# A four-layer stack on one Trainium2 core: image 1's first layer laid beside image 0's spline and attention, and a planner with other prices for TensorE

## The chip, the cores and the metric

The kernel runs on one core of a Trainium2 chip. The metric is the device time in microseconds of one execution, lower is better; the time before is 17189.96 us, the median of three runs (17174.03 to 17196.51).

## What is computed

An input of 32 images, each 128 channels by 56 x 56 pixels in float32, goes through four layers. Each adds its result to its input, and each first normalises its input over groups of four channels (`_gn`). Cut to what matters:

```python
# layer 0: a 1x1 convolution whose weights are mixed per image, then three depthwise convolutions
pooled = x.mean(axis=(2, 3)); attn = softmax(fc2(relu(fc1(pooled))) / 34)
y = einsum('boi,bihw->bohw', einsum('bk,koi->boi', attn, dw_weight), x) + attn @ dw_bias
out = sum(silu(depthwise3x3(y, dilation=d) + ds_bias) for d in (1, 3, 5))
# layer 1: a cubic B-spline of ten coefficients, the same for every element
basis = bspline_basis(clip(x, -2, 2), knots); out = einsum('...n,n->...', basis, coeffs)
# layer 2: linear attention over channels (8 heads, keys and queries from an 8x8 pooled image), depthwise 3x3
out = depthwise3x3(linear_attn(relu(pooled @ Wq.T), relu(pooled @ Wk.T), Wv x)) + bp
# layer 3: a Mamba block: layer norm, projections, convolution over 4, and a state space scan
h = exp(delta * A) * h + delta * B * xc      # 3136 steps, 16 states for each of 256 channels
y = sum_n(h * C) + xc * D;  out = out_proj(y * silu(z))
```

Images don't depend on each other. Within an image the layers follow each other, and the scan of layer 3 goes through the pixels in order.

## The kernel before

**Tiles.** An image is a tile `xt` of 128 channels by 3136 pixels; three such tiles rotate. Work is cut into seven chunks of 448 pixels (`CH`). The scan of a chunk takes 16 steps (`STEPS`): a step multiplies `du` with the B rows (`h<-du,pb`, VectorE), scans twice (`h<-da,last,h`, VectorE), multiplies by the C rows (`hc<-h,cb`, GpSimd) and sums over the states (`y<-hc,sums`, TensorE, added up in PSUM). The decay `da` is an Exp on ScalarE. `pb` is a float32r matmul into a PSUM tile with one buffer (`ps_bc`); `da` has three, `hc` two, and all other matmuls share the three buffers of `mm`.

**Stages.** A front part (lines 1256 to 1262) takes image 0 through layers 0, 1, 2 and the scan's first inputs, and image 1 through layer 0. Then a loop of five passes runs, each of six images, and after it two images are written out at the end. While the scan of image b runs, layers 1 and 2 of image b+1 (`until_scan`) and layer 0 of image b+2 (`first_layer`) are mixed in. Generators yield after each piece of work with its rough price, and `Pieces` doles the pieces out over the scan's 112 steps in proportion to those prices.

**Layer 0** (`dynamic_conv`) writes the mixed 1x1 convolution with a border to a DRAM image `padded[0]` and reads it back as stacks: for each chunk and dilation three shifted copies of the rows, laid over the partitions, and a row of ones for the bias. A stack is four DMAs on SyncE's queue (three of 264 KB and one of 8.2 KB), then twelve small matmuls (`mm<-stack,dsT`, four at a time in column groups), a Tanh (`t<-mm`, ScalarE), a product (`g`, VectorE) and an addition (`xt<-xt,g`, GpSimd). **Layer 1** (`spline`) reads each chunk as 16 DMAs of 56 KB (`stack<-xt`), makes hat functions on ScalarE (`hats`, one buffer) and sums them with 28 column-group matmuls in three groups (`mm<-hats,wspl`); two of the sums are squared on ScalarE (`sq`). **Layer 2** (`linear_attention`) has a chain of small matmuls (`wkT`, `wqT`, `wv`, then `bv`, `nm` and `kb` with 1 or 2 columns), eight heads that write `padded[1]`, and stacks of its own. All stacks of the three layers share one pool of three buffers (`stk`).

**The order.** `Plan` records every operation as a `Work` instead of issuing it (`add`), with the regions it reads and writes and a price in microseconds (`price`). `order` gives each work a due time: its scan step times 4.5 us, less its lead (`ahead`), or earlier where something due depends on it. `attempt` then plays the program forward with one clock for each engine: again and again it takes the work that can start first, of those of one engine the one that is due first, and sets that engine's clock on by the price. It lets no work be over 12 steps (`WINDOW`) ahead of the oldest undone one. `issue` writes all works out in the order of their planned starts, so each engine gets a fixed list that it follows in order; semaphores, not the plan's clock, decide when an instruction really runs. Every planned instruction carries line 325, where `issue` calls it, so the profile tells groups apart by tile names. The price of a matmul in the kernel before is in line 171:

```python
w.cost += max(0.06, n * (5e-4 if args[2].dtype == F32R else 1.8e-3))
```

where `n` is the number of columns. The plan is made once for the front, once for the loop's body and once for the last two images. `Pieces.finish` (line 1167) runs a generator to its end; with a plan it sets the step up by one for each piece.

Of the kernel before, what the change touches and what calls it, by code (L numbers as in the profile page):

```python
# [14 lines left out]
F32R = mybir.dt.float32r  # L15
# [4 lines left out]
P = 128  # L20
# [60 lines left out]
class Work:  # L81


    __slots__ = ("engine", "calls", "reads", "writes", "cost", "bytes", "step", "ahead", "table", "due", "next",
                 "ready", "fresh")

    def __init__(self, engine, step, ahead):
        self.engine, self.step, self.ahead = engine, step, ahead
        self.calls, self.reads, self.writes = [], [], []
        self.cost = self.bytes = self.ready = self.due = 0.0  # L90
        self.table = None
        self.next, self.fresh = [], []


class Plan:
# [6 lines left out]
    RATE, LANDING = 2e5, 1.8  # L102
    TABLE = 1.28
    NEVER = 1e18
    PATIENCE = {"tensor": 0.5, "scalar": 0.9, "gpsimd": 0.6, "vector": 0.1, "sync": 0.0}

    def __init__(self, nc, tc):
# [55 lines left out]
    def price(self, w, engine, method, args, kw):  # L163

        n = args[0].free_size()
        if method == "dma_start":
            w.cost += 0.35
            w.bytes += 4 * n * args[0].partition_size()
        elif engine == "tensor":
            n = args[2].free_size() if method == "matmul" else n  # L170
            w.cost += max(0.06, n * (5e-4 if args[2].dtype == F32R else 1.8e-3))
        elif engine == "scalar":
            if method == "activation" and args[2] in (AF.Exp, AF.Tanh, AF.Ln):
                w.table = "ln" if args[2] == AF.Ln else "exp"
            columns = sum(isinstance(kw.get(k), bass.AP) for k in ("bias", "scale"))
            w.cost += 0.06 + 8.34e-4 * n + 0.09 * columns + 0.03 * (args[1].space != bass.MemoryType.PSUM)
        elif engine == "gpsimd":
            if n <= 8:
                w.cost += 0.52 if ALU.pow in args else 0.15
            else:  # L180
                slow = method != "tensor_scalar" or ALU.add not in args
                w.cost += 0.14 + n * (1.2e-3 if not slow else 2.12e-3 if method != "tensor_scalar" else 3.8e-3)
        elif method == "tensor_tensor_scan":
            w.cost += 0.11 + 2.085e-3 * n
        else:
            if method == "tensor_reduce" or method == "bn_stats":
                n = args[1].free_size()
            w.cost += 0.08 + 1.02e-3 * n
# [54 lines left out]
    def attempt(self, born, behind):  # L243
# [6 lines left out]
        left = dict(self.uses)  # L250
        free = {e: 0.0 for e in self.PATIENCE}
        ready = {e: [] for e in self.PATIENCE}
        slots, held, table, bus, first = {}, {}, None, 0.0, 0
        for name, (pool, tag, bufs) in self.tiles.items():
            slots[pool, tag] = [0.0] * bufs
            held[pool, tag] = []
# [5 lines left out]
        while len(out) < len(works):  # L262
# [4 lines left out]
            for e, cand in ready.items():  # L267
                for i in cand:
                    w = works[i]
                    if w.step > front:  # L270
                        continue
                    at = max(w.ready, free[e])
                    for name in w.fresh:
                        at = max(at, min(slots[self.tiles[name][:2]], default=self.NEVER))
                    if at >= self.NEVER:
                        continue
# [11 lines left out]
            key, e, i, at = best  # L288
            w = works[i]
            ready[e].remove(i)  # L290
            done[i] = True
            for name in w.fresh:
                t = self.tiles[name][:2]
                slots[t].remove(min(slots[t]))
                held[t].append(name)
            free[e] = at + w.cost
            if w.table:
                free[e] += self.TABLE * (w.table != table)
                table = w.table
            end = free[e]  # L300
            if w.bytes:
                bus = max(bus, end) + w.bytes / self.RATE
# [12 lines left out]
                    ready[v.engine].append(k)  # L315
            out.append((at, i))
        return [i for _, i in sorted(out)]

    def issue(self):
        order, works = self.order(), self.works  # L320
# [29 lines left out]
def tile_conv_stack(ctx: ExitStack, tc: tile.TileContext, out: bass.AP, x: bass.AP, w: dict):  # L350
# [3 lines left out]
    plan = Plan(nc, tc)  # L354
# [770 lines left out]
    def first_layer(src, b):  # L1125

        xt = xts[b % 3]
        for j in range(NCH):
            nc.sync.dma_start(xt[:, j * CH : (j + 1) * CH], src[:, j * CH : (j + 1) * CH])
        yield from dynamic_conv(xt, sts[b % 2])  # L1130

    def until_scan(b):

        xt = xts[b % 3]
        st = yield from spline(xt, sts[b % 2])
        st = yield from linear_attention(xt, st)
        norm = carried[b % 2]
        norm_weights(st, *norm)
        yield 5.0
        layer_norm(xt, xns[b * NCH % 3], 0, norm)  # L1140
        yield 5.0

    def first_inputs(b):
        return ssm_inputs(xts[b % 3], b * NCH, carried[b % 2])
# [6 lines left out]
    class Pieces:  # L1151
# [12 lines left out]
            except StopIteration:  # L1164
                self.gen = None

        def finish(self, plan=None):
            while self.gen is not None:
                if plan is not None:
                    plan.at(plan.step + 1)  # L1170
                self.next()
            return self.taken

    xv = x.rearrange("b c l -> c b l")
# [79 lines left out]

    totals = [0.0, 0.0]
    plan.start()
    for b in range(2):
        totals[0] = Pieces(first_layer(xv[:, b : b + 1, :].squeeze(1), b)).finish(plan)
        if b == 0:
            totals[1] = Pieces(until_scan(0)).finish(plan)  # L1260
            Pieces(first_inputs(0)).finish(plan)
    plan.issue()
    with tc.For_i(0, B - 2, unroll) as i:
        images(i, unroll, True)
# [103 lines left out]
```

## Time and profile before

| | |
|---|---|
| median of three runs | 17189.96 us |
| profiled execution | 17194.07 us, its span 17192.1 us |
| busy: TensorE, VectorE, ScalarE, GpSimd | 14998.2, 14452.2, 11730.3, 10788.9 us |
| mean granted TensorE clock | 0.885 |
| first scan step (`h<-du,pb`) starts at | 508.6 us |
| images 0 to 29 (front's scan start to the last pass's end) | 508.6 to 16260.5 us, 525 us each |
| image 30, image 31 | 502.0 us, 429.6 us to the end of the span |

The profile is one execution. Busy time is given for each engine; TensorE's matmuls and weight loads (PEld) are told apart. A window row gives, for a stretch of the span, each engine's busy time with the number of its instructions, the granted TensorE clock as a share of full speed, and the share of the 16 DMA engines' time in use with GB/s. A wait row `A x <- B y` says how long engine A sat idle before its instruction on tile x until B's instruction on y released it. A float32 matmul stands as two records, a float32r matmul as one.

### The profile page before, as it was taken

To read this page: it belongs to the slowest core of one execution; us is meant where nothing else is said; L and a number is where in the kernel's file an instruction comes from. 1 tells how busy PE (TensorE), PEld (TensorE's weight loads), DVE (VectorE), ACT (ScalarE), POOL (GpSimd) and SP (SyncE) were. 2 spreads that over 40 slices of the span, in tenths; PEclk is the share of its full clock that TensorE was granted. 3 is DMA by queue.
4 is the path that set the end of the run, shared out by engine and by line. 5 is a ranking of instruction groups with operands and counts; after the bars stand their busy time and mean duration, and the time that the engine had idled before them with its cause. 6 is when DMAs were issued, how large, how long until landed. Compare 5 with 4: busy or idle time off the path is not lost. (4 is left out here: it accounts for less than half of the span.)

```text
span 17192.1 us, 216067 instructions
## 1 busy us (share of the span) xinstructions
PE 14998.2 (87%) x68192; PEld 4866.0 (28%) x68192; DVE 14452.2 (84%) x17314; ACT 11730.3 (68%) x21127; POOL 10788.9 (63%) x6406
## 2 busy tenths in 40 slices
PE   6888998888988888988889888889888898888888
PEld 1222222222222222222222222222222222222222
DVE  2788888888888888888888888888888888888889
ACT  3666677766677666777666776667776667766675
POOL 1566666666666666666666666666666666666666
PEclk7888898989998888989899888899888999888887
DMA  4443443434433444434344334444343443344421
GB/s 105 105 96 94 101 98 84 98 89 97 106 89 87 96 96 97 100 84 98 91 96 106 93 82 96 95 102 98 85 97 88 98 106 91 85 98 95 94 55 31
DMA packets 986167, 1590.09 MB, mean 92 GB/s; under 512 B 175621, under 2 KB 611208, under 8 KB 984330
## 3 DMA queue, kind: packets, MB, share of 16 engines
q1 hardware_dynamic: 985002, 1576.06, 39.0%
q8 instruction: 548, 8.98, 0.2%
q14 instruction: 617, 5.05, 0.1%
HBM read 785.62 MB, written 173.18 MB: 56 GB/s over the span
## 5 line engine op out<-in xcount | busy, mean ns | idle before, releaser
L325 POOL TENSOR_TENSOR hc<-h,cb 128x896 f32<-128x896 f32 x3584 | 7480.6, 2092 | 5035.7 <-DVE h L325 2490.3
L325 DVE TENSOR_TENSOR_SCAN h<-da,last,h 128x448 f32<-128x448 f32 x6144 | 6811.5, 1138 | 628.5 <-ACT da L325 530.6
L325 ACT ACTIVATE da<-delta,alog 128x448 f32<-128x448 f32 x7168 | 4490.6, 633 | 2043.6 <-DVE h L325 1843.0
L325 DVE TENSOR_TENSOR h<-du,pb 128x896 f32<-128x896 f32 x3584 | 3838.3, 1071 | 422.3 <-PE pb L325 179.9
L325 PE MATMUL y<-hc,sums 128*64 128x448 f32 x14336 | 3937.6, 628 | 283.7 <-POOL hc L325 279.3
L325 PE MATMUL pb<-dbl,sel 64*128 64x448 f32 x3584 | 1841.4, 514 | 626.6 <-DVE h L325 584.6
L325 PE MATMUL mm<-xn,winT 128*128 128x448 f32 x3584 | 1782.4, 605 | 172.0 <-DVE sz L325 129.5
L325 PE MATMUL mm<-stack,dsT 96*32 96x448 f32 (+1 forms) x16128 | 1877.0, 576 | 58.2 <-DMA stack<-onesd 23.5
L325 ACT ACTIVATE hats<-stack,bia,scl 128x448 f32<-128x448 f32 x2688 | 1894.2, 755 | 13.0 <-DVE bia L325 10.0
L325 PE MATMUL mm<-hats,wspl 128*32 128x448 f32 x12544 | 1476.4, 574 | 130.7 <-DVE xt L325 68.5
L325 PEld LDWEIGHTS pb<-dbl,sel 64*128 64x128 f32 x3584 | 714.6, 199 | 2985.3 <-DVE h L325 1877.5
L325 PEld LDWEIGHTS y<-hc,sums 128*64 128x64 f32 x14336 | 800.6, 146 | 2063.1 <-issue 971.8
L325 ACT ACTIVATE t<-mm 128x448 f32<-128x448 f32 x1568 | 816.5, 536 | 791.0 <-PE mm L325 780.4
L325 ACT COPY cb<-mm 128x448 f32<-128x448 f32 x1792 | 927.9, 529 | 568.0 <-PE mm L325 456.2
L325 PE MATMUL mm<-dbl,sel 64*128 64x448 f32 x1792 | 874.1, 517 | 476.1 <-ACT cb L325 139.4
L325 ACT ACTIVATE hats<-hats,one 128x1344 f32<-128x1344 f32 x896 | 1261.2, 1408 | 1.2
L325 ACT COPY last<-h 128x2 f32<-128x2 f32 x3072 | 579.0, 188 | 815.6 <-DVE h L325 790.3
L325 DVE TENSOR_TENSOR_SCAN h<-da,h 128x448 f32<-128x448 f32 x1024 | 1064.3, 1074 | 54.5 <-ACT da L325 46.5
L325 POOL TENSOR_TENSOR xt<-xt,g 128x448 f32<-128x448 f32 x672 | 765.1, 1139 | 341.9 <-DVE g L325 330.4
L325 PEld LDWEIGHTS mm<-xn,winT 128*128 128x128 f32 x3584 | 613.1, 199 | 1026.5 <-issue 662.5
L325 DVE SCALAR_TENSOR_TENSOR g<-t,mm 128x448 f32<-128x448 f32 x672 | 410.5, 611 | 406.1 <-ACT t L325 403.4
L325 PEld LDWEIGHTS mm<-stack,dsT 96*32 96x32 f32 (+1 forms) x16128 | 429.6, 113 | 1127.7 <-issue 875.2
(187 smaller groups left out, 15891.8 us busy)
## 6 DMA issues: line engine op xcount, KB each, us to landing
stack<-padded SPq DMA_DIRECT2D x2688, 264.0 KB
stack<-xt SPq DMA_DIRECT2D x3584, 56.0 KB
delta<-delta SPq DMA_DIRECT2D x1792, 112.0 KB
du<-du SPq DMA_DIRECT2D x1792, 112.0 KB
padded<-yc SPq DMA_DIRECT2D x224, 264.0 KB
padded<-yc SPq DMA_DIRECT2D x256, 231.0 KB
xt<-x_dram SPq DMA_DIRECT2D x224, 224.0 KB
out_dram<-xt SPq DMA_DIRECT2D x224, 224.0 KB
```

The source lines that it names most:

```text
L325: call()
```

## The change

It has two parts. In the front part, the layer 0 generator of image 1 is no longer run after image 0's first scan inputs. `finish` takes a second generator, `beside`, and after each piece of the first one takes pieces of the second until its summed prices have grown by half of what the first one has taken. Image 1's layer 0 thus gets the steps of image 0's spline and attention; what is left after these, and after the first scan inputs, follows.

In the planner, a float32r matmul is priced at 0.16 + 0.0005 n, any other at 0.02 + 0.00175 n but no less than 0.22. Each matmul also has a `load`, which grows with its columns and rows. `run` plays TensorE's clock in windows of 3.413 us (`GATE`): in a window that follows one with a load of 1.27 (`BUSY`) or more a work advances at full speed, else at half. The loop's program text is not touched, but its body and the last two images are ordered by the same planner. No instruction is added or removed.

```diff
--- before.py
+++ after.py
@@ -82,12 +82,12 @@
 
 
     __slots__ = ("engine", "calls", "reads", "writes", "cost", "bytes", "step", "ahead", "table", "due", "next",
-                 "ready", "fresh")
+                 "ready", "fresh", "load")
 
     def __init__(self, engine, step, ahead):
         self.engine, self.step, self.ahead = engine, step, ahead
         self.calls, self.reads, self.writes = [], [], []
-        self.cost = self.bytes = self.ready = self.due = 0.0
+        self.cost = self.bytes = self.ready = self.due = self.load = 0.0
         self.table = None
         self.next, self.fresh = [], []
 
@@ -102,6 +102,7 @@
     RATE, LANDING = 2e5, 1.8
     TABLE = 1.28
     NEVER = 1e18
+    GATE, BUSY = 3.413, 1.27
     PATIENCE = {"tensor": 0.5, "scalar": 0.9, "gpsimd": 0.6, "vector": 0.1, "sync": 0.0}
 
     def __init__(self, nc, tc):
@@ -168,7 +169,8 @@
             w.bytes += 4 * n * args[0].partition_size()
         elif engine == "tensor":
             n = args[2].free_size() if method == "matmul" else n
-            w.cost += max(0.06, n * (5e-4 if args[2].dtype == F32R else 1.8e-3))
+            w.load += n * (1.9e-4 if args[2].dtype == F32R else 7.5e-4 * 2) * args[-1 if method != "matmul" else 1].partition_size() / P
+            w.cost += 0.16 + 5e-4 * n if args[2].dtype == F32R else max(0.22, 0.02 + 1.75e-3 * n)
         elif engine == "scalar":
             if method == "activation" and args[2] in (AF.Exp, AF.Tanh, AF.Ln):
                 w.table = "ln" if args[2] == AF.Ln else "exp"
@@ -250,7 +252,7 @@
         left = dict(self.uses)
         free = {e: 0.0 for e in self.PATIENCE}
         ready = {e: [] for e in self.PATIENCE}
-        slots, held, table, bus, first = {}, {}, None, 0.0, 0
+        slots, held, table, bus, first, loads = {}, {}, None, 0.0, 0, {}
         for name, (pool, tag, bufs) in self.tiles.items():
             slots[pool, tag] = [0.0] * bufs
             held[pool, tag] = []
@@ -293,7 +295,7 @@
                 t = self.tiles[name][:2]
                 slots[t].remove(min(slots[t]))
                 held[t].append(name)
-            free[e] = at + w.cost
+            free[e] = self.run(at, w, loads) if e == "tensor" else at + w.cost
             if w.table:
                 free[e] += self.TABLE * (w.table != table)
                 table = w.table
@@ -315,6 +317,17 @@
                     ready[v.engine].append(k)
             out.append((at, i))
         return [i for _, i in sorted(out)]
+
+    def run(self, at, w, loads):
+
+        left = w.cost
+        while left > 0.0:
+            k = int(at / self.GATE)
+            speed = 1.0 if loads.get(k - 1, 0.0) >= self.BUSY else 0.5
+            stay = min((k + 1) * self.GATE + 1e-9 - at, left / speed)
+            loads[k] = loads.get(k, 0.0) + stay * speed * w.load / w.cost
+            at, left = at + stay, left - stay * speed
+        return at
 
     def issue(self):
         order, works = self.order(), self.works
@@ -1164,11 +1177,15 @@
             except StopIteration:
                 self.gen = None
 
-        def finish(self, plan=None):
+        def finish(self, plan=None, beside=None):
+
+            start = beside and beside.taken - self.taken / 2
             while self.gen is not None:
                 if plan is not None:
                     plan.at(plan.step + 1)
                 self.next()
+                while beside and beside.gen is not None and beside.taken - start < self.taken / 2:
+                    beside.next()
             return self.taken
 
     xv = x.rearrange("b c l -> c b l")
@@ -1254,11 +1271,11 @@
 
     totals = [0.0, 0.0]
     plan.start()
-    for b in range(2):
-        totals[0] = Pieces(first_layer(xv[:, b : b + 1, :].squeeze(1), b)).finish(plan)
-        if b == 0:
-            totals[1] = Pieces(until_scan(0)).finish(plan)
-            Pieces(first_inputs(0)).finish(plan)
+    layer0s = [Pieces(first_layer(xv[:, b : b + 1, :].squeeze(1), b)) for b in range(2)]
+    totals[0] = layer0s[0].finish(plan)
+    totals[1] = Pieces(until_scan(0)).finish(plan, layer0s[1])
+    Pieces(first_inputs(0)).finish(plan, layer0s[1])
+    layer0s[1].finish(plan)
     plan.issue()
     with tc.For_i(0, B - 2, unroll) as i:
         images(i, unroll, True)
```

## The prediction

> **What bounds the kernel now.** I read the page first (busy shares and granted clock), then windows by stage, then the waits of one pass of the loop. From the page:
>
> ```profile
> PE 14998.2 (87%) x68192; PEld 4866.0 (28%) x68192; DVE 14452.2 (84%) x17314; ACT 11730.3 (68%) x21127; POOL 10788.9 (63%) x6406
> ...
> PEclk7888898989998888989899888899888999888887
> ```
>
> Two engines stand at 84 and 87%, none at 100. The mean clock is 0.885; as the records hold only 1.0 and 0.5, (1 - 0.885) x 2 = 23% of the time is at half clock. So the bound is neither engine's work, but how the two in-order queues lie against each other. The windows of the front part (image 0's layer 0; its spline; its attention; norm and first scan inputs; image 1's layer 0) show another regime. Columns are named in the first line; a bracket is a count:
>
> ```profile
> core 0: us, PE busy (x) PEld busy (x) DVE busy (x) ACT busy (x) POOL busy (x), PEclk, DMA share, GB/s
> 38.00:138.00 100.00, 75.85 (x520) 23.10 (x519) 17.47 (x30) 15.68 (x28) 23.82 (x21) 0.80 0.88 200
> 138.00:298.00 160.00, 89.94 (x428) 19.32 (x428) 22.15 (x41) 99.98 (x127) 37.11 (x29) 0.65 0.15 36
> 298.00:369.00 71.00, 55.82 (x277) 24.50 (x277) 15.08 (x37) 11.21 (x20) 1.16 (x3) 0.72 0.49 130
> 369.00:404.00 35.00, 18.65 (x42) 9.38 (x42) 12.30 (x29) 15.13 (x21) 8.46 (x8) 0.70 0.06 14
> 404.00:508.60 104.60, 77.56 (x526) 24.66 (x526) 18.64 (x34) 18.19 (x33) 24.00 (x22) 0.79 0.90 206
> ```
>
> Layer 0 alone is bound by DMA (share 0.88 and 0.90); the spline by ACT and the matmul tail behind it (DMA 0.15). They ask for different things. The first scan step starts at 508.6. In the loop I cut image 7, an ordinary one, into its seven chunks of 16 scan steps:
>
> ```profile
> core 0: us, PE busy (x) PEld busy (x) DVE busy (x) ACT busy (x) POOL busy (x), PEclk, DMA share, GB/s
> 4188.70:4253.90 65.20, 48.95 (x160) 16.17 (x159) 59.97 (x79) 42.69 (x79) 44.23 (x25) 0.80 0.29 75
> 4253.90:4332.70 78.80, 62.92 (x251) 20.09 (x252) 67.41 (x86) 59.93 (x108) 48.81 (x30) 0.85 0.20 49
> 4332.70:4411.60 78.90, 73.68 (x349) 21.28 (x349) 64.05 (x71) 68.48 (x122) 54.59 (x34) 0.91 0.45 106
> 4411.60:4486.00 74.40, 67.53 (x367) 20.46 (x366) 63.24 (x73) 63.91 (x112) 55.83 (x34) 0.98 0.47 107
> 4486.00:4565.80 79.80, 71.30 (x322) 28.83 (x324) 67.01 (x82) 45.40 (x87) 42.89 (x27) 0.81 0.30 71
> 4565.80:4648.20 82.40, 81.33 (x454) 25.14 (x452) 69.87 (x82) 44.95 (x90) 46.08 (x27) 1.00 0.62 147
> 4648.20:4712.90 64.70, 57.09 (x233) 18.39 (x233) 59.08 (x70) 40.31 (x67) 44.56 (x28) 0.92 0.46 104
> ```
>
> Chunks 0 and 6 are DVE's (92 and 91%), chunk 5 is TensorE's (81.33 of 82.4). Chunks 1 to 4 belong to nobody: the busier engine of each makes 67.4, 73.7, 67.5 and 71.3, together 280 of 312 us. Thirty of the 32 images look like this, at 520 to 535 us. What ends DVE's idle time in one pass of the loop (images 12 to 17, 3147 us), total and count:
>
> ```profile
> DVE h L325 <- ACT da L325: 110.0, 84, 4.4
> DVE xt L325 <- PE mm L325: 49.8, 45, 2.3
> DVE g L325 <- ACT t L325: 49.8, 27, 4.5
> DVE h L325 <- PE pb L325: 31.6, 32, 2.7
> ...
> DVE rden L325 <- PE mm L325: 16.0, 6, 2.7
> DVE kb L325 <- PE mm L325: 13.8, 6, 2.3
> ```
>
> **What the skill says.** The Trainium skill, "TensorE: Matmul & The Clock Gate", Part 1, says that the clock has two states only and that activity in a free-running window of 3413 ns sets it. The trace agrees: its clock records are 1.0 or 0.5 and last whole multiples of 3413 ns (6827, 10240, 13653). The same page, Part 2, says that only the weight loads are pulled ahead, while matmuls stay in program order; so a matmul that waits holds all behind it. That is how I read the next row, TensorE's own waits in the same pass:
>
> ```profile
> PE pb L325 <- DVE h L325: 106.0, 117, 5.3
> ```
>
> "DMA: Bandwidth & Descriptors", "Issuing engines are not separate DMA queues", says that all queues share 16 DMA engines; in layer 0 alone they move 200 and 206 GB/s, in the spline 36, so there is room there. "Perfetto Trace Analysis", "Optimization Strategy", suggests interleaving regimes with different contended engines; no run here has shown yet what that gives.
>
> **Part 1, image 1's layer 0 beside image 0's spline.** No instruction is added or removed, only moved. In the new order 12 of its 21 stacks are issued before the last spline input and 9 after it; 16 of its 21 tanh stand between hats, 5 in the attention. Gross gain: the last du copies could be issued when du is made (403.3), the first four take 4 x 0.6 and land about 2 us later, so the scan could start at 408 instead of 508.6: 100 us. What hides the moved work: DMA, 104.6 x 0.90 = 94 us of work beside a spline and attention with (160 x 0.85) + (71 x 0.51) = 172 us free. ACT, 21 x 0.54 + 7 x 0.64 = 16 us, into 49.7 us in which ACT waits for matmuls (sq) in the spline. TensorE, 77 us, mostly while hats are made (160 - 90 = 70 us idle), and a warmer clock shortens the tail. What isn't hidden: SP's queue is in order, and its 84 layer-0 stack issues now stand between the 112 copies of the spline's input; both draw from the same three stack buffers, two of which hold spline input. Nine stacks are issued after the last spline input; at 104.6 / 21 = 5 us each that is 45 us, against some 20 us of spline and 27 us of attention start. ACT is in order too: a tanh whose stack is late holds the hats. I charge 35 us, between 5 (all hidden) and 80 (each of 7 chunks held by 10 us). **Net -65.**
>
> **Part 2, prices and half clock in the plan.** This changes no instruction of the loop, only the order. The float32r matmul was priced at 448 x 0.0005 = 0.224 us; back to back at full clock the trace has 0.40, and the new price is 0.384. Matmuls of 1 to 4 columns were 0.06, now 0.22. In half-clock windows everything counts double. The new rule (window before under a load of 1.27) laid over the trace's own matmuls and clock records gives the right state in 89 of 100 windows; "always full", as the old plan has it, in 77. So the plan comes nearer to the chip. What it does to one pass, by mean places on TensorE's queue: pb 1.0 earlier, the attention's chain (wv 18, kb 10, the denominators 7) earlier; the C rows 2.0, winT 1.3, wzT 2.4 later; y 0.5 later. On ACT da goes 0.5 earlier, cb 1.2 later. DVE's scans hardly move (0.1).
>
> Those that move earlier are waited for: pb 31.6 + rden 16.0 + kb 13.8 = 61.4 us a pass, 10.2 an image. I take half of it, 5.1, since part of these waits is TensorE's load, which stays. Bounds: all waits of DVE that go back to a matmul, directly or through ACT (xt, g, pb, delta 29.1, sz 22.8, rden, kb and smaller ones), are 245 us a pass, 41 an image; a third of that, 13.6, is the most I credit. On the other side the earlier pb can cost (rival B), 6.4 an image. The C rows that go back hide behind their lead of two steps (AHEAD); if that cover is gone POOL waits, which has 36% idle. The last image has no side work, so 31 images count: 31 x 5.1 = **-158.**
>
> **Sum**, against the profiled execution (17194.07, span 17192.1, 2 us around it, 4 above the median 17189.96): 17194 - 65 - 158 = 16971, say **16970**.
>
> **Rivals.**
> A, the front only: the loop's new order gains here and loses there. For it: half of all neighbours on TensorE's queue stay as they were, chunks 0, 5 and 6 are bound by work. Against: chunks 1 to 4 have 32 us free. 17194 - 65 = 17129. Chance 0.19.
> B, **slower**: pb has one PSUM buffer, so a pb placed ahead waits for DVE's multiply, and TensorE is held with it (the 106.0 above). Where TensorE is the bound, chunks 2 and 5, that is lost time: 32 steps, half of them, 0.4 us each (one matmul's place) = 6.4 an image, 205 in all; 17194 - 65 + 205 = 17334. It decides from (65 + 34) / 32 = 3.1 us an image. Against: in these chunks DVE runs ahead of TensorE, and the ready pb is what the scan needs. Chance 0.15.
> C, the better price pays throughout: a third of the 41 us, 13.6 x 31 = 422; 16707. Chance 0.20.
> That the half-clock rule doesn't do what it says would be A. My forecast has 0.46.
>
> **Range and chances.** About 0.2%, 34 us, is what a measurement can tell from no change. Range 16700 to 17225: half of C falls below, two thirds of B above. Faster: forecast, C and two thirds of A, 0.79; within: 0.08 from the rims of A, B and the forecast; slower 0.13.
>
> **What would show it.** Right: the first scan step near 443, DMA share in the spline above 0.5 and its clock above 0.65; images near 519 with chunk 4 shortest against before; "DVE h <- PE pb", "rden" and "kb" smaller. Wrong: "PE pb <- DVE h" above 106 a pass and chunks 2 and 5 longer (B); a spline stage over 200 us (ACT held by late stacks).

## The result and the profile after

The changed kernel takes 17130.50 us (median of eight runs, 17116.74 to 17140.79) against 17184.10 us of the kernel before in the same session: ratio 0.997, 95% interval 0.9961 to 0.9979. It is 0.3% faster. The forecast was 1.3%, 16970 us; the number that came lies next to rival A's, 17129.

The page of the execution profiled after (17116.74 us, span 17115.0) hardly differs from the one before. TensorE and VectorE are busy about as long as they were, and the mean clock is 0.887 against 0.885:

```profile
PE 15011.9 (88%) x68192; PEld 4886.0 (29%) x68192; DVE 14420.9 (84%) x17314; ACT 11725.0 (69%) x21127; POOL 10795.2 (63%) x6406
...
PEclk7888899888898988988889988889998899888987
```

So I cut the span at the first scan step, at the end of image 29 and at the end of image 30. All stage times below are cuts at the starts of `h<-du,pb` in one profiled execution.

| | before, us | after, us | difference |
|---|---|---|---|
| front, up to the first scan step | 508.6 | 434.3 | -74.3 |
| loop, images 0 to 29 | 15751.9 | 15777.4 | +25.5 |
| image 30 | 502.0 | 482.7 | -19.3 |
| image 31, to the end | 429.6 | 420.5 | -9.1 |

The whole gain lies outside the loop. The two profiled executions are 77.2 us apart, the medians only 53.6: the one before lies 10 us above its session's median, the one after 14 below. Five profiled executions with this end or nearly so (the change, e2, e7, e13 and e16 below) agree within 2.4 us in it, and the four of them with this front within 8 in that, so the spread lies mostly in the loop. An estimate from the medians is then that the loop lost 49 us (74.3 + 28.4 - 53.6), twice what the table shows.

**The front.** The windows of after (image 0's layer 0; its spline with image 1's layer 0; attention; attention's end; the scan's first inputs):

```profile
core 0: us, PE busy (x) PEld busy (x) DVE busy (x) ACT busy (x) POOL busy (x), PEclk, DMA share, GB/s
38.00:140.00 102.00, 76.62 (x537) 25.23 (x537) 25.23 (x56) 17.48 (x32) 24.43 (x22) 0.83 0.90 210
140.00:300.00 160.00, 103.36 (x738) 32.23 (x738) 28.41 (x55) 101.29 (x137) 49.55 (x40) 0.75 0.56 132
300.00:369.00 69.00, 63.75 (x341) 24.84 (x345) 16.46 (x31) 21.94 (x36) 11.92 (x12) 0.73 0.47 112
369.00:404.00 35.00, 21.48 (x151) 7.78 (x143) 9.35 (x19) 6.69 (x9) 2.48 (x4) 0.89 0.46 114
404.00:434.30 30.30, 14.10 (x28) 6.28 (x28) 3.46 (x7) 11.08 (x16) 6.18 (x6) 0.67 0.22 49
```

Set the second row against the spline's row of before: the DMA share goes from 0.15 to 0.56, the clock from 0.65 to 0.75, and there is no row of 104.6 us at 206 GB/s left. The first hat starts at 145.0 instead of 142.8 and the last ends at 307.5 instead of 284.2, 23.3 us later, and nearly all that the move costs is paid there. ScalarE's waits between these two points, before (L325) and after (L338):

```profile
ACT sq L325 <- PE mm L325: 42.6, 12, 7.1
ACT sq L338 <- PE mm L338: 35.6, 12, 8.6
ACT yc L338 <- DMA padded<-yc: 9.5, 1, 9.5
ACT t L338 <- PE mm L338: 8.8, 5, 7.9
```

Sixteen tanhs of image 1 and five `yc` of the attention now stand between the hats. They add 10.3 us of work and 18.3 us of waiting, and the wait for `sq` is 7.0 shorter: together 21.6, about the 21.1 us by which the hats are stretched.

**The loop.** Image 7 of after, by its seven chunks:

```profile
core 0: us, PE busy (x) PEld busy (x) DVE busy (x) ACT busy (x) POOL busy (x), PEclk, DMA share, GB/s
4116.70:4184.70 68.00, 49.57 (x166) 16.40 (x164) 60.11 (x78) 42.57 (x78) 44.67 (x25) 0.80 0.26 66
4184.70:4264.80 80.10, 65.85 (x259) 20.29 (x258) 65.64 (x87) 62.29 (x112) 49.80 (x31) 0.84 0.23 59
4264.80:4342.70 77.90, 72.50 (x351) 21.93 (x347) 63.28 (x72) 66.61 (x118) 56.56 (x35) 0.90 0.43 101
4342.70:4416.90 74.20, 69.35 (x358) 21.34 (x358) 63.33 (x73) 63.51 (x112) 52.83 (x33) 0.91 0.44 102
4416.90:4493.60 76.70, 70.71 (x324) 28.57 (x325) 67.74 (x83) 44.68 (x86) 43.28 (x27) 0.87 0.34 80
4493.60:4573.30 79.70, 79.37 (x448) 25.24 (x446) 69.10 (x82) 44.86 (x92) 45.15 (x26) 1.00 0.61 145
4573.30:4642.80 69.50, 61.18 (x236) 19.44 (x236) 60.02 (x71) 41.67 (x68) 45.03 (x29) 0.88 0.46 104
```

Chunk 4 fell from 79.8 to 76.7 and chunk 5 from 82.4 to 79.7; chunks 0 and 6 rose from 65.2 to 68.0 and from 64.7 to 69.5. The means of images 6 to 29 say the same: 65.5, 78.4, 78.6, 73.9, 79.5, 82.0, 66.8 became 67.8, 80.1, 77.1, 73.5, 76.3, 79.8, 71.4. The order was rearranged, and the image keeps its length (524.7 and 525.9 in the mean). VectorE's idle time moved in the same way: per image it rose from 5.2 to 7.3 us in chunk 0, from 10.6 to 13.6 in chunk 1 and from 7.1 to 10.4 in chunk 6, and fell from 11.8 to 7.9 in chunk 4 and from 11.2 to 9.5 in chunk 5. All seven chunks together have 71.4 us of it, where they had 69.7. What VectorE waited for in one pass (images 12 to 17, 3157 us):

```profile
DVE h L338 <- ACT da L338: 105.7, 65, 5.0
DVE xt L338 <- PE mm L338: 59.9, 50, 3.3
DVE h L338 <- PE pb L338: 56.7, 52, 3.3
DVE g L338 <- ACT t L338: 36.1, 14, 4.8
...
DVE h L338 <- POOL rstd L338: 14.1, 4, 3.5
...
DVE kb L338 <- PE mm L338: 6.8, 6, 1.4
...
DVE rden L338 <- PE mm L338: 6.0, 6, 1.5
```

The attention's waits (`rden`, its denominators, and `kb`) fell from 29.8 to 12.8 us, as the forecast had it. The wait for pb rose from 31.6 to 56.7; by chunks of images 6 to 29 it is new in chunk 4 (0 to 4.7 us an image) and chunk 6 (0.1 to 2.7) and smaller in chunks 0 to 2. And TensorE's own wait in front of pb, 106.0 before, went up too:

```profile
PE pb L338 <- DVE h L338: 130.9, 143, 5.5
```

Three of the new stalls can be followed, the last only in part. In chunk 4's step 15 of image 7, TensorE's timeline:

```profile
4483.32 1.76 PE L338 MATMUL y<-hc,sums 128*64 128x448 f32 x4
4485.01 4.40 PE L338 MATMUL mm<-stack,dsT 97*32 97x448 f32 x24
4489.34 0.47 PE L338 MATMUL pb<-dbl,sel 64*128 64x448 f32 x1
```

and VectorE's beside it:

```profile
4483.50 1.09 DVE L338 TENSOR_TENSOR h<-du,pb 128x896 f32<-128x896 f32 x1 [0.25 <-PE pb L338]
4484.69 2.19 DVE L338 TENSOR_TENSOR_SCAN h<-da,last,h 128x448 f32<-128x448 f32 x2
4489.91 1.09 DVE L338 TENSOR_TENSOR h<-du,pb 128x896 f32<-128x896 f32 x1 [3.03 <-PE pb L338]
```

The depthwise group in front of pb takes 4.40 us; the same 24 records take 2.48 at full clock. Ahead of it TensorE had run the attention's matmuls of 1 and 2 columns, and the clock was at half (PEclk 0.50) from 4475.31 to 4488.96:

```profile
4475.31:4488.96 13.65, 13.51 (x72) 8.31 (x70) 7.29 (x10) 8.29 (x15) 8.01 (x5) 0.50 0.46 102
```

Whether those small matmuls brought the clock down was not tried. In images 6 to 29 this one wait is 2.7 us an image. The second stall is in chunk 6, which lost most. In its step 7 of image 6 the multiply waits 1.85 us for a pb that stands behind depthwise records, two of `winT` and a `y`:

```profile
4070.71 3.21 PE L338 MATMUL mm<-stack,dsT 96*32 96x448 f32 x16
4073.85 1.86 PE L338 MATMUL mm<-xn,winT 128*128 128x448 f32 x2
4075.64 1.10 PE L338 MATMUL y<-hc,sums 128*64 128x448 f32 x4
4076.67 0.47 PE L338 MATMUL pb<-dbl,sel 64*128 64x448 f32 x1
```

In images 6 to 29 this wait is 2.0 us an image. The third stall is at the end of chunk 0, in 16 of these 24 images: `h<-du,pb` waits 3.53 us and the trace names GpSimd's `rstd`.

```profile
4172.14 1.28 ACT L338 ACT_TABLE_LOAD   x1
4173.44 0.58 ACT L338 ACTIVATE rstd<-rstd 128x448 f32<-128x448 f32 x1
4173.92 2.05 ACT L338 ACTIVATE hats<-stack,bia,scl 128x448 f32<-128x448 f32 x3
4175.87 0.18 ACT L338 COPY last<-h 128x2 f32<-128x2 f32 x1
```

ScalarE's copy `last` ends at 4176.05, the multiply starts at 4176.14. The copy reads an `h`, of which there are three buffers, and it stood behind a table load, `rstd` and three hats. That it and not `rstd` released the multiply is argued from the code, not shown.

### The profile page after: what moved, and what is told of

It is laid out like the page before. It is cut to its first block, busy times and chain, and to the rows that moved or that the text cites. A ratio compares the mean times of both kernels' runs of the same rounds, so it can differ in the third digit from the quotient of the medians.

```text
span 17115.0 us, 216293 instructions
## 1 busy us (share of the span) xinstructions
PE 15011.9 (88%) x68192; PEld 4886.0 (29%) x68192; DVE 14420.9 (84%) x17314; ACT 11725.0 (69%) x21127; POOL 10795.2 (63%) x6406
## 5 line engine op out<-in xcount | busy, mean ns | idle before, releaser
L338 POOL TENSOR_TENSOR hc<-h,cb 128x896 f32<-128x896 f32 x3584 | 7485.4, 2094 | 4739.4 <-DVE h L338 1971.9
L338 DVE TENSOR_TENSOR_SCAN h<-da,last,h 128x448 f32<-128x448 f32 x6144 | 6784.5, 1137 | 564.4 <-ACT da L338 454.1
L338 ACT ACTIVATE da<-delta,alog 128x448 f32<-128x448 f32 x7168 | 4499.6, 634 | 2452.5 <-DVE h L338 2210.7
L338 DVE TENSOR_TENSOR h<-du,pb 128x896 f32<-128x896 f32 x3584 | 3841.3, 1072 | 692.5 <-PE pb L338 307.6
L338 PE MATMUL y<-hc,sums 128*64 128x448 f32 x14336 | 3948.4, 635 | 392.1 <-POOL hc L338 388.9
L338 PE MATMUL pb<-dbl,sel 64*128 64x448 f32 x3584 | 1860.5, 519 | 801.3 <-DVE h L338 722.1
L338 PE MATMUL mm<-stack,dsT 96*32 96x448 f32 (+1 forms) x16128 | 1950.1, 595 | 44.2 <-DMA stack<-onesd 21.3
L338 ACT ACTIVATE hats<-stack,bia,scl 128x448 f32<-128x448 f32 x2688 | 1880.0, 754 | 29.8 <-DVE bia L338 15.5
L338 PE MATMUL mm<-xn,winT 128*128 128x448 f32 x3584 | 1840.5, 623 | 67.1 <-DVE sz L338 43.6
L338 PEld LDWEIGHTS pb<-dbl,sel 64*128 64x128 f32 x3584 | 715.9, 200 | 3031.3 <-DVE h L338 1998.0
L338 PE MATMUL mm<-hats,wspl 128*32 128x448 f32 x12544 | 1449.3, 569 | 71.6 <-DVE xt L338 34.1
L338 ACT ACTIVATE t<-mm 128x448 f32<-128x448 f32 x1568 | 812.9, 537 | 944.4 <-PE mm L338 921.3
L338 PEld LDWEIGHTS y<-hc,sums 128*64 128x64 f32 x14336 | 797.0, 147 | 2039.9 <-issue 969.0
L338 ACT ACTIVATE hats<-hats,one 128x1344 f32<-128x1344 f32 x896 | 1261.8, 1408 | 0.6
L338 ACT COPY cb<-mm 128x448 f32<-128x448 f32 x1792 | 928.9, 529 | 360.4 <-PE mm L338 235.3
L338 DVE TENSOR_TENSOR_SCAN h<-da,h 128x448 f32<-128x448 f32 x1024 | 1063.4, 1073 | 104.1 <-ACT da L338 95.3
L338 PE MATMUL mm<-dbl,sel 64*128 64x448 f32 x1792 | 874.2, 511 | 272.6 <-DVE g L338 110.3
L338 POOL TENSOR_TENSOR xt<-xt,g 128x448 f32<-128x448 f32 x672 | 766.4, 1140 | 452.4 <-DVE g L338 419.6
L338 ACT COPY last<-h 128x2 f32<-128x2 f32 x3072 | 580.1, 189 | 596.3 <-DVE h L338 577.6
L338 PEld LDWEIGHTS mm<-xn,winT 128*128 128x128 f32 x3584 | 625.3, 203 | 947.6 <-issue 726.8
L338 PEld LDWEIGHTS mm<-stack,dsT 96*32 96x32 f32 (+1 forms) x16128 | 446.2, 115 | 1180.9 <-issue 951.1
L338 PEld LDWEIGHTS mm<-dbl,sel 64*128 64x128 f32 x1792 | 353.7, 208 | 1249.5 <-issue 343.4
```

The source lines that it names most:

```text
L338: call()
```

## The experiments

All fifteen runs in one table; time and ratio are medians, the ratio to the kernel before on the same chip, with its 95% interval. The last three columns come from one profiled execution of each kernel, which can lie 30 us off the median (17095.55 against 17125.66 in e15, 17227.05 against 17197.60 in e2). "End" is images 30 and 31.

| run | us | ratio | front | loop | end |
|---|---|---|---|---|---|
| before | 17184.10 | | 508.6 | 15751.9 | 931.5 |
| the change | 17130.50 | 0.997 (0.9961 to 0.9979) | 434.3 | 15777.4 | 903.3 |
| e1_front | 17141.58 | 0.9978 (0.9972 to 0.9985) | 437.7 | 15740.2 | 940.8 |
| e2_plan | 17197.60 | 1.0011 (1.0004 to 1.0018) | 502.3 | 15820.2 | 902.7 |
| e3_prices | 17050.14 | 0.9927 (0.9910 to 0.9943) | 438.6 | 15709.4 | 913.1 |
| e4_clock | 17219.02 | 1.0026 (1.0015 to 1.0036) | 432.4 | 15881.4 | 914.3 |
| e5_floor | 17107.16 | 0.9958 (0.9942 to 0.9975) | 437.9 | 15729.6 | 929.8 |
| e6_f32r | 17105.59 | 0.9951 (0.9935 to 0.9968) | 440.4 | 15755.5 | 921.3 |
| e7_mixed | 17100.51 | 0.9953 (0.9936 to 0.9970) | 437.1 | 15753.3 | 904.3 |
| e8_uniform | 17437.90 | 1.0149 (1.0132 to 1.0166) | 439.8 | 16087.3 | 915.1 |
| e9_phase1 | 17048.64 | 0.9923 (0.9907 to 0.9940) | 440.8 | 15709.4 | 905.7 |
| e10_phase2 | 17124.88 | 0.9964 (0.9954 to 0.9973) | 431.6 | 15789.2 | 897.7 |
| e11_p18 | 17062.85 | 0.9931 (0.9915 to 0.9948) | 438.4 | 15729.8 | 912.6 |
| e12_p14 | 17128.66 | 0.9965 (0.9951 to 0.9979) | 438.1 | 15781.4 | 916.4 |
| e13_pb79 | 17110.70 | 0.9957 (0.9941 to 0.9974) | 442.0 | 15765.5 | 903.6 |
| e15_busy | 17125.66 | 0.9968 (0.9956 to 0.9981) | 439.6 | 15735.2 | 918.9 |
| e16_pb_g | 17183.35 | 0.9999 (0.9990 to 1.0008) | 435.3 | 15844.8 | 905.1 |

All diffs below are against the changed kernel.

### The change in its parts

Theory: the front gives its gain by itself, and the loop's gain failed to come. Rival: the parts need each other.

**e1_front**: the new front, the old planner.

```diff
-            w.cost += 0.16 + 5e-4 * n if args[2].dtype == F32R else max(0.22, 0.02 + 1.75e-3 * n)
+            w.cost += max(0.06, n * (5e-4 if args[2].dtype == F32R else 1.8e-3))
...
-            free[e] = self.run(at, w, loads) if e == "tensor" else at + w.cost
+            free[e] = at + w.cost
```

> The new front with the old planner: prices and clock as before, so the loop and the last two images are ordered as before. Theory (the front is the whole gain, the loop's new order is a wash): first scan step near 434 to 445, loop 15752 as before, last two images 931.5, in all about 17120. Rival (the loop gains or loses with what lies in front of it): the loop differs from 15752 by over 15 us although its order is the same.

**e2_plan**: the old front loop over the two images with the new planner.

```diff
-    layer0s = [Pieces(first_layer(xv[:, b : b + 1, :].squeeze(1), b)) for b in range(2)]
-    totals[0] = layer0s[0].finish(plan)
-    totals[1] = Pieces(until_scan(0)).finish(plan, layer0s[1])
-    Pieces(first_inputs(0)).finish(plan, layer0s[1])
-    layer0s[1].finish(plan)
+    for b in range(2):
+        totals[0] = Pieces(first_layer(xv[:, b : b + 1, :].squeeze(1), b)).finish(plan)
+        if b == 0:
+            totals[1] = Pieces(until_scan(0)).finish(plan)
+            Pieces(first_inputs(0)).finish(plan)
```

> The new planner with the old front. Theory: first scan step near 505 to 510, loop 15777 as after the change, last two images 903, in all within 0.1% of before. Rival (the new planner is worth something that the new front eats up): the loop is shorter than 15752.

The front's place is worth 0.22% by itself; the planner by itself costs 0.11%. In e2 the end gains 28.8 us and the front 6.3, and the loop loses 68.3 in the profiled execution, 54 by the estimate from medians (18.6 + 28.8 + 6.3). That agrees with the change's 49, so the 43 us between the two profiled loops are spread of one order, and e2's rival, a loop shorter than 15752, is out.

In e1 less than the front's gain arrives. The scan starts 70.9 us earlier, but the median is only 37.4 below that of the kernel before; its profiled execution, the fastest of twenty, hides this. The end takes 9.3 us more there, and some 24 us, an estimate, must have gone in the loop, though its order is the old one. So e1's rival, a loop that depends on what lies in front of it, is not out. Nor do the parts quite add up: 0.9978 x 1.0011 = 0.9989, and the change has 0.997.

**e3_prices** takes the half clock out of the plan (the second hunk of e1), **e4_clock** takes the new prices out (the first).

> The whole change without the half clock: TensorE always at full speed in the plan, the new prices kept. Theory (the prices gain in chunk 4, the half clock loses in chunks 6, 0 and 1): loop 3 to 8 us an image shorter than after the change, some 15550 to 15690. Rival (the prices lose, pb put too early): loop as long as after the change or longer, 15777 and up.

> The whole change with the old prices: the half clock alone. Theory (the half clock loses): loop longer than 15777, chunk 4 as long as before (79.5 us), chunks 6 and 0 as long as after (71 and 68). Rival (the half clock gains, the prices lose): loop under 15752.

With the prices alone the kernel is 0.7% faster, with the half clock alone 0.26% slower, although both have the new front. Against e1, which has the new front too, the prices bring 0.51%, and the half-clock rule on top of them takes back 0.43%. But neither theory's places came. e3's loop, 15709.4, missed its 15550 to 15690, and its chunk 1 rose to 84.8 us. e4's chunks 6 and 0 are as long as before (66.9 and 65.5 us, where 71 and 68 were expected), and its loss is in chunk 5 (86.7 for 82.0). So the change's longer chunks 0 and 6 come from neither part alone. The 0.43% could be a fault of the rule, or it could be that each planner only gives another order, some good and some bad. The next two groups ask this.

### Is a nearer model a better order?

**e8_uniform** has the new prices and, in place of the half clock, makes every work of TensorE slower by 5.5%.

```diff
-            free[e] = self.run(at, w, loads) if e == "tensor" else at + w.cost
+            free[e] = at + w.cost * (1.055 if e == "tensor" else 1.0)
```

> The new prices, and in place of the half-clock windows the plan's mean loss by them (5% of TensorE's time in its plan of the loop) on every TensorE work alike. Theory (the harm is in the places where the plan puts its half-clock windows, not in a slower TensorE): as fast as the prices alone, 17050 give or take 30. Rival (a slower TensorE as such harms, because pb and the fillers are put elsewhere): as slow as the whole change, 17130.

It is 1.5% slower than before; both views are wrong by over 300 us. Against e3 every chunk but 1 and 3 is longer (chunk 2 by 3.4, chunk 6 by 5.0 us). A change of 5.5% in one engine's prices moved the loop by 378 us; why so far is open.

**e9_phase1** and **e10_phase2** keep everything of the change and only let the plan's windows of 3.413 us begin 1.1 or 2.3 us earlier. The model is neither nearer nor farther by that.

```diff
-            k = int(at / self.GATE)
+            k = int((at + 1.1) / self.GATE)
...
-            stay = min((k + 1) * self.GATE + 1e-9 - at, left / speed)
+            stay = min((k + 1) * self.GATE - 1.1 + 1e-9 - at, left / speed)
```

> The whole change with its windows of 3.413 us begun 1.1 us earlier, a third of a window: the same rule, other places. Theory (the places are wrong anyway, since the chip's windows aren't tied to the plan's zero): between 17080 and 17230, in chance order, and over 25 us away from the whole change. Rival (half-clock pricing as such costs some 80 us): 17130 give or take 20.

> The same with the windows begun 2.3 us earlier, two thirds of a window. Theory: again somewhere between 17080 and 17230, not where the third of a window lies. Rival: 17130 give or take 20.

17048.64, 17124.88 and, unshifted, 17130.50: the phase alone moves the time by 80 us, more than the whole change. e9 is even below the 17080 that its theory allowed, and e10 fits the rival as well. The Trainium skill, "TensorE: Matmul & The Clock Gate", Part 1, calls the chip's window free-running. The traces agree: counted from the first instruction, the bounds of their clock records lie between 0.05 and 3.38 us into a window of 3.41, at another place in each of the seventeen. So the plan cannot know the phase. The runs show how far another place of the plan's windows moves the time; they don't show that any place is the right one.

**e15_busy** has 1.7 for `BUSY`. The planner, played by itself, then puts 19% of the loop's windows at half clock instead of 10.7%; the chip has (1 - 0.893) x 2 = 21%.

> The whole change with 1.7 in place of 1.27 as the load that a window needs for a full clock. The plan of the loop then has 19% of its windows at half clock (10.7% with 1.27); the chip has 21%. Theory (the plan gains when its share of half clock is the chip's): below 17100, with the pb wait after the attention's small matmuls gone from chunk 4. Rival (the share may be right while the places of the half windows are not, so this is one more draw): anywhere from 17050 to 17220, and the loop no shorter than 15709.

17125.66: the chip's share brings nothing over 17130.50. The wait for pb in chunk 4 stayed (4.20 us an image, 4.69 in the change). The theory fell; the rival, one more draw, fits.

### Which price?

**e5_floor** has only the floor of 0.22 for small matmuls, **e6_f32r** only the float32r price, **e11_p18** and **e12_p14** have both with 0.18 and 0.14 for 0.16; none has the half clock.

```diff
+            w.cost += 5e-4 * n if args[2].dtype == F32R else max(0.22, 1.8e-3 * n)
...
+            w.cost += 0.16 + 5e-4 * n if args[2].dtype == F32R else max(0.06, 1.8e-3 * n)
...
+            w.cost += 0.18 + 5e-4 * n if args[2].dtype == F32R else max(0.22, 0.02 + 1.75e-3 * n)
```

> Theory (the floor of 0.22 us for matmuls of 1 to 4 columns is what moved the attention's chain earlier and shortened chunk 4): the denominators' and kb waits fall as in the whole change (rden from 2.7 to under 1.5 us an image), mean chunk 4 near 77, loop near 15710 as with both prices; time near 17055. Rival (the gain comes from the float32r price): chunk 4 stays near 79, loop near 15740, time near 17085 or above. Third view (each price list is only another draw of the order): the loop lands anywhere within 15700 to 15830, with no tie to those waits.

> The other half of the prices alone: float32r matmuls at 0.16 + 0.0005 n, the small ones still at 0.06. Theory (the floor matters): chunk 4 near 79, rden waits near 2.7 us an image, loop near 15740, time near 17085. Rival (the float32r price is the one that matters): loop near 15710, time near 17055. If floor and float32r price add up, this run's loop and that of the floor alone have gains against 15746 that sum to about 37 us, the gain of both prices together. If they don't, by more than 40 us, the orders are draws.

> The prices alone with 0.18 in place of 0.16 us ahead of a float32r matmul's columns: a price as good as the other (0.404 against 0.40 in the trace). Theory that the better prices are what pays: within 30 us of the prices alone, 17050. Rival that any new order is a draw of some tens of us either way: over 40 us from it.

> Both prices without the half clock, 0.14 in place of 0.16 for a float32r matmul. Theory (prices near the measured ones give a better order): within 20 us of the runs with 0.16 and 0.18, so 17040 to 17080. Rival (each price list is a draw of about half a per cent): 17000 to 17180, as likely beyond those 20 us as within.

The floor does half of what it was thought to do in its place: chunk 4 is 76.9 (79.5 before) and kb's wait is gone, but rden's is 2.5 us an image, where less than 1.5 was expected (2.7 before); with the float32r price alone chunk 4 stays at 78.8 and rden's wait rises from 2.7 to 4.2 us an image. But against the old order's loop (15752, 15740 and 15753 in three executions, mean 15748) the floor gains 19 us, the float32r price loses 7, and both together gain 39. They don't add up, though the 27 us between stay under the 40 that e6 had set as its mark and are near what two executions of one order can differ. e5's time, 17107, lies above its theory's 17055, and e6's, 17106, above both of its views. The step from 0.16 to 0.18 costs 20 us in the loop, and e11 came within its theory's 30 us of e3; the step to 0.14 costs 72, and e12 is 79 us above e3, where its rival alone allows it. A price near the measured one is not safe by that.

### The loop left as it was

**e7_mixed** plans the front and the last two images with the new planner and the loop's body with the old one: `new` is set to False ahead of the loop and back after it.

```diff
+            if self.new:
+                w.cost += 0.16 + 5e-4 * n if args[2].dtype == F32R else max(0.22, 0.02 + 1.75e-3 * n)
+            else:
+                w.cost += max(0.06, n * (5e-4 if args[2].dtype == F32R else 1.8e-3))
...
+            free[e] = self.run(at, w, loads) if e == "tensor" and self.new else at + w.cost
```

> New planner for the front and for the last two images, old planner for the loop's body. Theory (front and last two images are gains of their own, the loop is where the forecast gain failed to come): 434 + 15746 + 903 = 17083, so 17070 to 17100, below the whole change's 17130. Rival (the last two images only gain because the loop before them has the new order too): near 17141, as with the new front alone.

17100.51, half a microsecond above the theory's range, with 437.1, 15753.3 and 904.3 us: front and end gain without the loop's new order. This is the plainest sign that the change's gain doesn't come from its loop. Here too less arrives than the stages give: 80.7 us by medians, 98.7 in front and end.

### Taking the new wait away

**e13_pb79** moves pb of chunk 4's step 15 ahead of the depthwise group in the finished order. `name` is a work's first written tile, `queue` TensorE's order, `queue[j:k]` the group in front of work `i`.

```diff
...
+            if name(i) == "pb" and k > j and self.works[i].step % 112 == 77:
+                group = queue[j:k]
+                order = [x for x in order if x not in group]
+                at = order.index(i) + 1
+                order[at:at] = group
```

> The whole change, with one edit of the finished order: in every image the pb of chunk 4's step 15 goes ahead of the depthwise group (12 matmuls, 4.40 us in the trace, half clock) that stands before it. Theory (this wait is loop time that the new order added): VectorE's wait there, 2.7 us an image, goes, chunk 4 is shorter by 2 to 2.7, chunk 5 as before, so 60 to 80 us off 17130: 17050 to 17070. Rival (chunk 5 belongs to TensorE, so VectorE's head start is waited for again at the next pb): chunk 4 shorter by about 2, chunk 5 longer by about 2, time within 20 us of 17130.

The wait at pb went from 2.73 to 0.41 us an image, and chunk 4 didn't get shorter (76.3 and 77.0; loop 15765.5). VectorE in the same step shows where it went:

```profile
4490.84 1.09 DVE L354 TENSOR_TENSOR h<-du,pb 128x896 f32<-128x896 f32 x1 [0.41 <-POOL hc L354]
4494.58 0.62 DVE L354 SCALAR_TENSOR_TENSOR g<-t,mm 128x448 f32<-128x448 f32 x1 [2.65 <-ACT t L354]
4495.11 2.18 DVE L354 TENSOR_TENSOR_SCAN h<-da,last,h 128x448 f32<-128x448 f32 x2
```

The multiply starts almost at once (the 0.41 is a wait for hc), but g, which reads the same group's tanh, is next in VectorE's queue, ahead of the scans. It waits 2.65 us, 2.5 in the mean. The time, 17110.70, is 20 us below the change's, where the theory asked for 60 to 80. The rival's time is met, its longer chunk 5 is not (79.9 for 79.8).

**e16_pb_g** therefore also moves this g behind the two scans (six products a pass; `at` as above).

```diff
+                    late = [x for x in order[at:] if self.works[x].engine == "vector"]
+                    m = next(x for x in late if name(x) == "g")
+                    scans = late[late.index(m) + 1:][:2]
...
+                        order.remove(m)
+                        order.insert(order.index(scans[1]) + 1, m)
```

> The whole change with pb moved as in the run before, and the product g that reads the same depthwise group's tanh moved behind the two scans of its step on VectorE. Theory (the 2.7 us an image was waited for at pb, then at g in the same step; with both out of VectorE's way it is gained): chunk 4 shorter than in the run with pb alone by 2 to 2.6, chunk 5 as before, so the loop near 15700 and the time near 17045. Rival (TensorE's group at half clock is work that chunk 5 waits for anyway, at the next pb, hc or y): chunk 5 longer by about as much, time within 20 us of 17111.

```profile
4504.81 1.09 DVE L361 TENSOR_TENSOR h<-du,pb 128x896 f32<-128x896 f32 x1 [0.41 <-POOL hc L361]
4506.01 2.19 DVE L361 TENSOR_TENSOR_SCAN h<-da,last,h 128x448 f32<-128x448 f32 x2
4508.56 0.62 DVE L361 SCALAR_TENSOR_TENSOR g<-t,mm 128x448 f32<-128x448 f32 x1 [0.36 <-ACT t L361]
4511.82 1.09 DVE L361 TENSOR_TENSOR h<-du,pb 128x896 f32<-128x896 f32 x1 [2.65 <-POOL hc L361]
```

Now g waits 0.36, and the next multiply 2.65 (2.2 in the mean). Chunk 4 is still 77.0. The multiply was released by hc (in some images the trace names a stack's DMA, but in the twelve looked at, 6 to 17, hc ended 0.03 to 0.04 us before the multiply); GpSimd's rows show what hc waited for, TensorE's where that stood:

```profile
4502.70 2.08 POOL L361 TENSOR_TENSOR hc<-h,cb 128x896 f32<-128x896 f32 x1 [2.32 <-PE y L361]
4509.70 2.09 POOL L361 TENSOR_TENSOR hc<-h,cb 128x896 f32<-128x896 f32 x1 [4.92 <-PE y L361]
```

```profile
4503.21 4.71 PE L361 MATMUL mm<-stack,dsT 97*32 97x448 f32 x24
4507.85 1.76 PE L361 MATMUL y<-hc,sums 128*64 128x448 f32 x4
4509.54 0.62 PE L361 MATMUL mm<-dbl,sel 64*128 64x448 f32 x1
4509.54 0.62 PE L361 MATMUL pb<-dbl,sel 64*128 64x448 f32 x1
```

The y that frees hc's buffer stands behind the same depthwise group: 4.71 us of group, 1.76 of y, 2.09 of hc, then the multiply at 4511.82. The next pb, at 4509.54, is no earlier than that y. So the wait was handed on twice, from pb to g to hc, and the scan steps after it start no earlier. TensorE has no gap in this stretch; whatever goes ahead of the group, something else of TensorE's is late. I read that as TensorE at half clock being the bound here. To move y and the next pb ahead as well was not tried.

The rival's mechanism held, though in the same chunk and through hc; its time (within 20 us of 17111) did not: the run is 73 us slower, with chunk 6 longer by 1.9 us, chunk 3 by 0.8 and chunk 6's granted clock at 0.850 against 0.883. Against e13 one product an image was moved, in chunk 4, and the clock two chunks on was another; by which chain is open.

## Why the prediction was right and wrong

**Part 1, the front: right in its own stage.** Forecast -65, measured -74.3 (-70.9 in e1, -71.5 in e7). The first scan step came at 434.3, forecast near 443. Of 100 us gross 25.7 were lost where 35 were charged, in the spline, as argued: what now stands between the hats in ScalarE's queue, its work and its waits, makes 21 of the 23.3 us. The bound of 80 us never came near. The Trainium skill, "Perfetto Trace Analysis", "Optimization Strategy", on interleaving regimes with different contended engines, is borne out in this stage: DMA share 0.56 in the spline, and the scan starts 74 us earlier. In the whole execution e1 shows only 37.4 us of it; what takes the rest in the loop is open, and the forecast had no term for it.

**Part 2, the loop: wrong.** The term was -158, 31 images of 5.1. Measured: +25.5 for 30 images (some 49 by the medians) and -19.3 for image 30. The step that failed is "Those that move earlier are waited for ... I take half of it". Of the three waits in that sum, rden and kb fell by 17.0 us a pass, more than half of their 29.8. The third, pb, went the other way by 25.1, so the sum of the three rose from 61.4 to 69.5. I had read "pb 1.0 earlier" on TensorE's queue as earlier in time. A place in a queue is no time: what stands ahead of it can be slower (4.40 us for 2.48), and the new order has other things ahead of the pb of chunks 4 and 6. The new prices alone (e3) give 2.4 us of pb wait an image in chunk 4 and 0.5 in chunk 6, the half clock alone (e4) none in either, both together 4.7 and 2.7.

Below that lies a second mistake, which e3, e13 and e16 show: I took waits of VectorE as time that a better order gives back. e3 waits for pb as long as the change does (10.2 and 10.1 us an image, 5.3 before), and its loop is 68 us shorter. In chunk 4 a wait of 2.7 us an image was removed at pb, came back at g, was removed there and came back at the next multiply, by way of y and hc. So chunk 4, one of the four that I had called nobody's, has a stretch in which TensorE at half clock has no gap, though no engine is full over the chunk. The same is not shown for chunks 1 to 3.

**"So the plan comes nearer to the chip": true in part, and no reason for a gain.** The rule gave 89% of the windows of the trace before, but the planned loop had half the chip's share of half clock. A recount over that loop gives 88% with 1.27 for `BUSY`, 93% with 1.5 and 92% with 1.7, so e15's rule fits the trace better still, and sets the share right, and it brought nothing; moving the phase (e9, e10), which comes no nearer, moved the time by 80 us. Ten different new orders (e2 and the change counted as one at their mean, without e8 and the two moved by hand) have loops of 15709 to 15881 us, mean 15762, with a standard deviation of 53 (15758 and 53 if each is set right by its median); the old order has 15748. With e8, the one far outside, it is 15792 and 110. From these runs a new model's order is a draw of at least 0.3% either way, with no sign that it is better on the whole. A small gain by the prices is not excluded: the five loops with new prices and no half clock have a mean of 15741, the five with the half clock 15783, each group with a range of 70 us or more.

**The signs.** Spline's DMA share above 0.5 and clock above 0.65: both came. Chunk 4 shortest against before: came (-3.2). Images near 519: no, 525.9. "DVE h <- PE pb" smaller: no, 56.7 for 31.6; rden and kb smaller: came. "PE pb <- DVE h" above 106 stood for rival B, and it is 130.9; but B placed the loss in chunks 2 and 5, and these are shorter (78.6 to 77.1, 82.0 to 79.8). The loss is in chunks 0, 1 and 6 (2.3, 1.7 and 4.6 us).

**The rivals.** A's time, 17129, was 1.5 us off, and that is luck: it starts from one execution (17194.07) that lies 10 us above the median, and errors cancel in part. By the stage cuts the front gave 9 us more than in A, the loop lost 25.5, and the end, which I gave no term of its own, gained 28.4. Why the end gains under every new planner (1.7 us in e5, 33.8 in e10, 15 to 19 with both prices alone) was not tried. C is not reached by any run; the best, e9 and e3, are at 17049 and 17050, 0.5% below the changed kernel. Whether that is more than a lucky order is not shown: e10 differs from e9 only in the phase and e12 from e3 only in one digit, and they are 76 and 79 us slower.

## What to carry to other kernels

Price a move in a stage with one clear bound from its windows: here that sum held within 10 us for the stage, while e1's median kept only half of it. So look at the whole execution as well, by medians and not by one profile. Where two in-order engines take turns, don't book a wait as a gain: ask what that engine, and the one it waits for, would meet next, and look whether the slower one has any gap in that stretch, at the clock it has there. And when a planner's prices are changed, measure a few neutral variations (a phase, a third digit) first: if they move the time as far as the change does, one run of the change can't tell a better model from another draw.

## What the runs showed that I had not expected

- One order can take different times in the loop in two executions: 15740, 15752 and 15753 us for the old one, 15777 and 15820 for the new. The eleven executions of e10, one kernel, lie between 17077 and 17150 us.
- Over the sixteen profiled executions without e8's the loop's time and its mean granted clock go together, correlation -0.80; over the eleven executions of e10 the whole time and the mean clock have -0.98. Which drives which is open: by the rule that gave 89% of the windows a stall, which leaves a window emptier, would slow what follows, and slower work would make the next stall.
- A depthwise group of 24 records takes 2.48 us at full clock and up to 4.71 at half clock (4.40 in the stall of chunk 4, which ran into the full clock at its end).
